# Three shared-expert products as seven products of halves, and routed sums moved ahead of a conditional block

## The chip, the cores and the metric

The kernel runs on one core of a Trainium2 chip. The metric is the device time of one execution in microseconds (us). The times of the kernel before are three runs: 1027.62, 1027.80 and 1028.35 us, median 1027.8 us. Times in tables of the trace are microseconds from the start of the profiled span.

TensorE (PE) multiplies matrices, VectorE (DVE), ScalarE (ACT) and GpSimd (POOL) do elementwise work, SyncE (SP) issues most of the DMAs, POOL issues the indirect ones (gathers). Each engine works through its own instructions in the order in which the program gives them; an instruction that waits holds up everything behind it on its engine.

## The reference, cut to what matters

Input is x of shape (4, 512, 512) in float32. A modulated layer norm leads to a block with a time mix and a channel mix, and then to a mixture of experts. Only this last part matters here:

```python
sh_mid = gelu(einsum('th,ehd->ted', xt, Wsh_up))          # 2 shared experts, 512 -> 256
shared_out = einsum('ted,edh->th', sh_mid, Wsh_down)      # 256 -> 512, summed over both
probs = softmax(xt @ W_router)
top_v, top_i = top_k(probs, 2)                            # of 16 routed experts
rt_mid = gelu(einsum('th,ehd->ted', xt, Wrt_up))
routed_out = einsum('ted,edh->th', rt_mid * gate[:, :, None], Wrt_down)
...
x = x + gb * (shared_out + routed_out)
```

## The kernel before, in words

A batch is 512 tokens, four row tiles of 128 (`NT = 4`), with `H = 512` features, `T = 512` tokens, half size `HT = 256`. The program runs: the time mix of the four batches, the channel mix of the four batches (its large products are already done as seven products of halves), and the experts. Nothing reorders the work: the order of every engine's instructions is the order of the Python code.

**Shared experts.** `shared_up(b)` computes, for the four 128-row pieces of the two experts' middle layer, four matmuls each with a 128x512 result, 16 in all, and a Gelu into a `mid` tile. `shared_down(b)` computes, for four row tiles, four matmuls with a 128x512 result, again 16 in all; `scaled_onto` (L1177, L1178) multiplies by the batch's gate row and adds onto x. Both are generators: each `yield` gives back control, so that their steps can be put between other work. Of the eight shared products, `shared_up(0)`, `shared_up(1)` and `shared_down(0)` are woven into the last channel mix. The other five belong to the part looked at here.

**Routed experts.** Tokens are sorted into slots of 128 rows, each with one expert's weights. 41 slots always run (`N_FIRST`), six more only if the device's count says so (the `tc.If` at L1426; it was not taken in this execution). A slot passes through five steps: `turn` (gathered rows are transposed, L1222, copied by DVE, L1224), `up` (8 records of 256-wide matmuls, Gelu), `turn_mid` (L1238, L1240), `down` (4 records of 512-wide matmuls, ACT copy), `keep` (a DMA stores the rows to `y_d`). Each step of slot s stands beside the previous step of slot s+1. Weights and rows are fetched three slots ahead.

**Fillers.** Every second pass of the slot loop from s = 22 on also runs one step of `groups`, which chains `shared_down(1)` and `shared_up(2)`, four steps each. In the passes s = 41 to 44, which drain the slots, it runs one step of `last_ups`, which is `shared_up(3)`. `gather(b, t)` fetches each token's two routed rows from `y_d` with two indirect DMAs; `routed(b, t)` combines them (ACT scales one, L1292; DVE L1293, then `scaled_onto`). For batches 0 and 1 this is done between the slots; `gather(2, ...)` is issued in the passes s = 43 and 44.

**The end.** After `last_ups` comes the conditional block, then `gather(3, ...)` (eight indirect DMAs on POOL), then the shared down products of batches 2 and 3. There `routed_and` (L1300, L1301) adds the two gathered rows straight to the product in PSUM, then `scaled_onto`, then a store. The very last row tile (b = 3, t = 3) has its routed part added earlier by `routed`, and its product is made in two halves of 256 columns in one PSUM bank (L1444), with a DVE multiply and add for each half (L1452, L1453) and a store of each half.

PSUM has eight banks, four with the tag "ps" and four with the tag "acc".

**The conditional block in the built program.** Every engine passes the `If`. On the path that is not taken, an engine waits until its own instructions so far are done, and then raises its count by what the block would have raised it by. The first matmul behind the block waits for DVE's count as it stands after this, that is, for a DVE that has itself finished everything ahead of the block and has passed it. This holds in the program before (where DVE's last instruction ahead of the block is the copy L1240 of slot 40) and in the changed one.

**The front.** In the time mix of batch 1, `weave` runs steps of `time_front(2)` between the steps of the main work; a plan says how many per main step. The step `n(3)` there makes the last normalized tile `xn_ln` (L219 on ACT) which PE then transposes (L226).

Of the kernel before, what the change touches and what calls it, by code (L numbers as in the profile page):

```python
# [10 lines left out]
AF = mybir.ActivationFunctionType  # L11
# [3 lines left out]
P = 128  # L15
# [29 lines left out]
def adaln_block(  # L45
# [1100 lines left out]
    def shared_up(b, halves=False):  # L1146
        mids[b] = []
        for wu, _ in shared:
            for m in range(ND):
                ps = bank(f"ps_up_sh_{b}_{len(mids[b])}")  # L1150
                for k in range(NK):
                    nc.tensor.matmul(  # L1152
                        ps, wu[:, k, m * P : (m + 1) * P], h3s[b][k], start=(k == 0), stop=(k == NK - 1)
                    )
                    if halves and k % 2:
                        yield
                act = row_tile(f"mid_{b}_{len(mids[b])}", (P, T))
                nc.scalar.activation(act, ps, AF.Gelu)
                mids[b].append(act)
                if not halves:  # L1160
                    yield
        h3s[b] = None

    def down_products(b, t, ps, js):
        for j in js:
            nc.tensor.matmul(  # L1166
                ps,
                mids[b][j][:, t * P : (t + 1) * P],
                shared[j // ND][1][:, j % ND, :],
                start=(j == 0),  # L1170
                stop=(j == len(mids[b]) - 1),
            )
# [115 lines left out]
    def routed(b, t):  # L1288

        g0, g1 = gates_of(b, t)  # L1290
        y0, y1 = got.pop((b, t))
        nc.scalar.activation(y1, y1, AF.Copy, scale=g1)  # L1292
        nc.vector.scalar_tensor_tensor(y0, y0, g0, y1, ALU.mult, ALU.add)  # L1293
        scaled_onto(b, t, y0)

    def routed_and(b, t, ps):

        g0, g1 = gates_of(b, t)
        y0, y1 = got.pop((b, t))
        nc.vector.scalar_tensor_tensor(y0, y0, g0, ps, ALU.mult, ALU.add)  # L1300
        nc.vector.scalar_tensor_tensor(y0, y1, g1, y0, ALU.mult, ALU.add)  # L1301
        scaled_onto(b, t, y0)
# [65 lines left out]
    for b in range(1, B):  # L1368
        if b + 1 < B:
            back = chained(lambda: time_front(b + 1))  # L1370
        else:
            wcr = load_w(wcr_t, "wcr")
            loaded[0] = load_keys(0, 0)
            back = front_and_sums()
            gas[0] = spread(GA, 0)
        weave(time_mix(b), back, (2, 1, 2, 1, 2) if b == 1 else ())
        drain(back)
# [27 lines left out]
    groups = chained(lambda: shared_down(1), lambda: shared_up(2))  # L1405
    last_ups = shared_up(B - 1)
    at = [slots_by(b) + 5 for b in range(B - 1)]
    for s in slots(0, N_FIRST, ready):
        if s >= slots_by(0) - 1 and (s - slots_by(0)) % 2:
            next(groups, None)  # L1410
# [13 lines left out]
    drain(last_ups)  # L1424
    n_used = nc.values_load(used[0:1, 0:1], min_val=0, max_val=N_SLOT)
# [4 lines left out]
    for b in (B - 2, B - 1):  # L1430
        for t in range(NT):
            ps = down_bank(b, t)
            if b == B - 1 and t == NT - 1:
                break
            down_products(b, t, ps, range(4))
            if b == B - 1 and t == NT - 2:
                routed(b, NT - 1)
            routed_and(b, t, ps)
            store_out(b, t)

    last = x1s[B - 1][NT - 1]
    for at in (slice(0, HT), slice(HT, H)):
        for j in range(4):
            nc.tensor.matmul(  # L1444
                ps[:, at],
                mids[B - 1][j][:, (NT - 1) * P :],
# [4 lines left out]
        add = row_tile(f"add_last_{at.start}")  # L1451
        nc.vector.tensor_mul(add[:, at], ps[:, at], gbs[B - 1][:, at])  # L1452
        nc.vector.tensor_add(last[:, at], last[:, at], add[:, at])  # L1453
# [45 lines left out]
```

## Time and profile before

| | |
|---|---|
| median of the runs | 1027.8 us (1027.62 to 1028.35, 3 runs) |
| the profiled execution | 1028.34 us, of it a span of 1026.5 us; 1.84 us lie around the span |
| busy in the span | PE 98%, DVE 60%, ACT 31%, POOL 33% |
| PE waiting, the two largest sums | L226 for ACT's `xn_ln` 6.5 us (5 times), L1444 for DVE's `add_last` 3.3 us (once) |
| granted TensorE clock | 0.997 over the span |
| DMA | 178 GB/s over the span; 382 GB/s and PE busy throughout at 800 to 825 us, 268 to 326 GB/s at 875 to 950 us |

The trace can be read line by line: a line of the timeline gives the start, the duration, the engine, the source line, the operation with output and inputs, the shape, and how many instructions of the kind followed each other; in brackets stands how long the engine had been idle, and what ended that. A float32 matmul leaves two records. The durations of single matmuls overlap, so the pace of PE is read from starts, not from durations.

### The profile page before, as it was taken

The numbers are of one execution on the slowest core, as the hardware profiler recorded it, in microseconds if no ns is written. First come the engines' busy times: TensorE is split into PE (matmuls) and PEld (weight loads), VectorE is DVE, ScalarE is ACT, GpSimd is POOL, SyncE is SP. The second block draws the span as 40 slices with busy tenths as digits, with TensorE's granted clock in tenths as the row PEclk, the third lists the DMA queues.
The fourth block names the chain that finished last, engine by engine and source line by source line (L and its number), as shares of the span: only waits on it lengthen the run. The fifth ranks groups of instructions, "written<-read, shape, count | busy, mean of one in ns | idle before, by whom it ended". The sixth has DMA issues, their size and how long they took to land. (4 is left out here: it accounts for less than half of the span.)

```text
span 1026.5 us, 11651 instructions
## 1 busy us (share of the span) xinstructions
PE 1003.0 (98%) x3930; PEld 685.8 (67%) x3930; DVE 616.8 (60%) x1181; ACT 319.8 (31%) x530; POOL 342.3 (33%) x324
## 2 busy tenths in 40 slices
PE   7999999999999999999999999999998999999997
PEld 2444444444688888888888888888646676666643
DVE  5787887797665736848757587428654222233426
ACT  1765645653222305320262203220021222122310
POOL 2463563514354105620266006520104221232160
PEclk9999999999999999999999999999999999999999
DMA  9600401352069562365226534650536999899762
GB/s 328 247 0 2 125 19 42 103 192 86 1 225 349 178 233 83 121 232 178 88 76 215 195 133 175 240 180 1 185 123 187 365 382 383 270 321 316 266 194 83
DMA packets 96765, 182.83 MB, mean 178 GB/s; under 512 B 7528, under 2 KB 50280, under 8 KB 92608
## 3 DMA queue, kind: packets, MB, share of 16 engines
q1 hardware_dynamic: 90864, 162.92, 45.6%
q0 software_dynamic: 5840, 19.14, 5.8%
q8 instruction: 32, 0.52, 0.2%
q14 instruction: 29, 0.24, 0.1%
HBM read 149.75 MB, written 32.29 MB: 177 GB/s over the span
## 5 line engine op out<-in xcount | busy, mean ns | idle before, releaser
L199 POOL TENSOR_TENSOR rstd_ln<-rstd_ln,minus_half 128x1 f32<-128x1 f32 x64 | 42.9, 672 | 199.5 <-DVE rstd_ln L198 182.5
L782 PE MATMUL ps_y<-wval,a 128*128 128x256 f32 x384 | 86.0, 380 | 0.0
L1207 POOL DMA_INDIRECT xg<-h_d,token x41 | 39.5, 963 | 127.9 <-PE ps_xt L1222 44.8
L782 PEld LDWEIGHTS ps_y<-wval,a 128*128 128x128 f32 x384 | 72.3, 190 | 12.0 <-issue 2.5
L1230 PE MATMUL ps_up<-wrt,xt 128*128 128x256 f32 x328 | 78.0, 381 | 0.3 <-ACT act L1232 0.2
L1246 PE MATMUL ps_down<-wrt,at 128*128 128x512 f32 x164 | 77.2, 593 | 0.0
L1230 PEld LDWEIGHTS ps_up<-wrt,xt 128*128 128x128 f32 x328 | 59.1, 190 | 8.0 <-DVE xt L1224 1.0
L1224 DVE COPY xt<-ps_xt 128x512 f32<-128x512 f32 x41 | 28.2, 689 | 56.2 <-PE ps_xt L1222 42.1
L711 PE MATMUL ps_ky<-T,keys_hi 128*128 128x256 f32 x256 | 60.6, 380 | 0.0
L711 PE MATMUL ps_kx<-mix_ln,keys_lo 128*128 128x256 f32 x256 | 60.5, 379 | 0.0
L357 PE MATMUL ps_o<-wo,av 128*128 128x512 f32 x128 | 57.4, 597 | 2.4 <-DVE x L427 1.2
L352 PE MATMUL ps_r<-mix_ln,wr 128*128 128x512 f32 x128 | 57.6, 593 | 0.8 <-issue 0.8
L782 PE MATMUL ps_z<-wval,a 128*128 128x256 f32 x256 | 57.9, 380 | 0.0
L352 PE MATMUL ps_v<-mix_ln,wv 128*128 128x512 f32 x128 | 57.5, 592 | 0.0
L782 PE MATMUL ps_x<-wval,a 128*128 128x256 f32 x256 | 57.2, 379 | 0.0
L1152 PE MATMUL ps_up_sh<-h,wsh 128*128 128x512 f32 x128 | 57.2, 593 | 0.0
L394 DVE RECIPROCAL p<-p 128x512 f32<-128x512 f32 x16 | 53.6, 3353 | 0.6
L1166 PE MATMUL ps_down_sh<-wsh,mid 128*128 128x512 f32 x120 | 53.1, 595 | 0.3 <-PEq L1426 0.3
L711 PEld LDWEIGHTS ps_kx<-mix_ln,keys_lo 128*128 128x128 f32 x256 | 48.5, 190 | 6.9 <-issue 0.5
L711 PEld LDWEIGHTS ps_ky<-T,keys_hi 128*128 128x128 f32 x256 | 48.3, 190 | 6.8 <-DVE ku L749 0.4
L782 PEld LDWEIGHTS ps_z<-wval,a 128*128 128x128 f32 x256 | 48.1, 190 | 6.8 <-issue 0.6
L782 PEld LDWEIGHTS ps_x<-wval,a 128*128 128x128 f32 x256 | 48.2, 190 | 6.3
(260 smaller groups left out, 1845.3 us busy)
## 6 DMA issues: line engine op xcount, KB each, us to landing
wrt<-in_rt_up_dram SPq DMA_DIRECT2D x41, 512.0 KB
wrt<-in_rt_down_dram SPq DMA_DIRECT2D x41, 512.0 KB
wval<-sums_d SPq DMA_DIRECT2D x16, 1024.0 KB
wval<-in_wval_t_dram SPq DMA_DIRECT2D x12, 1024.0 KB
keys_lo<-keys_d SPq DMA_DIRECT2D x12, 1024.0 KB
y_d<-y SPq DMA_DIRECT2D x41, 256.0 KB
keys_hi<-keys_d SPq DMA_DIRECT2D x12, 768.0 KB
mod<-mod_d SPq DMA_DIRECT2D x22, 256.0 KB
```

The lines of the kernel that those rows point to most:

```text
L199: nc.gpsimd.tensor_tensor(rstd, rstd, minus_half, ALU.pow)
L352: nc.tensor.matmul(ps, w[:, k, m * P : (m + 1) * P], acts[k], start=(k == 0), stop=(k == NK - 1))
L357: nc.tensor.matmul(ps, acts[k][:, t * P : (t + 1) * P], w[:, k, :], start=(k == 0), stop=(k == NK - 1))
L394: nc.vector.reciprocal(p, p)
L711: nc.tensor.matmul(ps[:, c * HT : (c + 1) * HT], w[:, k, c * P : (c + 1) * P], acts[k], start=(fresh and c == 0 and k == 0), stop=(c == 1 ...
L782: nc.tensor.matmul(ps[:, j * HT : (j + 1) * HT], acts[p][:, c, j * P : (j + 1) * P], w[:, i, :], start=(fresh and i == 0 and j == 0), stop ...
L1152: nc.tensor.matmul(ps, wu[:, k, m * P : (m + 1) * P], h3s[b][k], start=(k == 0), stop=(k == NK - 1))
L1166: nc.tensor.matmul(ps, mids[b][j][:, t * P : (t + 1) * P], shared[j // ND][1][:, j % ND, :], start=(j == 0), stop=(j == len(mids[b]) - 1),)
L1207: nc.gpsimd.indirect_dma_start(out=xg, out_offset=None, in_=h3_d, in_offset=bass.IndirectOffsetOnAxis(ap=token[:, s : s + 1], axis=0),)
L1224: nc.vector.tensor_copy(xt.rearrange("p k t -> p (k t)"), ps)
L1230: nc.tensor.matmul(ps[:, :D], xt[:, k, :], wu[:, k, :], start=(k == 0), stop=(k == NK - 1))
L1246: nc.tensor.matmul(ps, at[:, j, :], wd[:, j, :], start=(j == 0), stop=(j == ND - 1))
```

## The change

1. `shared_down(1)`, `shared_up(2)` and `shared_up(3)` become `shared_down_seven` and `shared_up_seven`: each is cut into 2 x 2 halves and computed with seven products of halves (four 256-wide matmuls each, 28 in all) in place of eight (16 matmuls of width 512), with DVE additions of the partial results.
2. The sums of halves that this needs are made ahead: `shared_sums()`, eight DVE additions of 128x512, in the pass s = 3 of the slot loop; `shared_down_terms(1)` (four of 128x512) at s = 19, `shared_up_terms(2)` (eight of 128x256) at s = 27, `shared_up_terms(3)` (eight of 128x256) at s = 37.
3. In `shared_down_seven`, DVE multiplies by the gate row, and POOL adds the halves of 128x256 onto x.
4. The middle tiles of batches 0 and 1 are written per half of the tokens: two Gelus of 256 columns instead of one of 512.
5. The plan of the weave in the time mix of batch 1 becomes (2, 2, 1, 2).
6. `routed(2, t)` for all four t, with DVE also doing the scaling (`tensor_scalar`), moves ahead of the conditional block. `routed_and` goes: behind the block, each product gets a `scaled_onto` alone, and `routed(3, t)` (scaling on ACT) follows the store of each tile of batch 2.
7. The two halves of the last row tile get a PSUM bank each.

```diff
     def shared_up(b, halves=False):
-        mids[b] = []
+        mids[b] = [[row_tile(f"mid_{b}_{t}_{f}", (P, ND, HT)) for f in range(E_SH)] for t in range(2)]
...
-                act = row_tile(f"mid_{b}_{len(mids[b])}", (P, T))
-                nc.scalar.activation(act, ps, AF.Gelu)
+                for t in range(2):
+                    nc.scalar.activation(mids[b][t][f][:, m, :], ps[:, t * HT : (t + 1) * HT], AF.Gelu)
...
+    def shared_sums():
...
+        add(ups, "S1", "A21", "A22", ALU.add)
+        add(ups, "S2", "S1", "A11", ALU.subtract)
+        add(ups, "S3", "A11", "A21", ALU.subtract)
+        add(ups, "S4", "A12", "S2", ALU.subtract)
+        add(downs, "T1", "B12", "B11", ALU.subtract)
+        add(downs, "T3", "B22", "B12", ALU.subtract)
+        add(downs, "T2", "B22", "T1", ALU.subtract)
+        add(downs, "T4", "B21", "T2", ALU.subtract)
...
+    def seven(name, product, A, Bs, use):
+        X = bank(f"{name}_x")
+        product(X, A["A11"], Bs["B11"], True)
+        c1 = copied(f"{name}_c1", X)
+        Y = bank(f"{name}_y", "acc")
+        product(Y, A["S2"], Bs["T2"], True)
+        u = row_tile(f"{name}_u")
+        nc.vector.tensor_add(u, c1, Y)
+        yield
+        Z = bank(f"{name}_z", "acc")
+        product(Z, A["S1"], Bs["T1"], True)
+        c5 = copied(f"{name}_c5", Z)
+        nc.vector.tensor_add(c5, c5, c1)
+        product(X, A["A12"], Bs["B21"], False)
+        use(0, 0, X)
+        yield
+        product(Y, A["S3"], Bs["T3"], False)
+        nc.vector.tensor_add(c5, c5, Y)
+        use(1, 1, c5)
+        product(Z, A["S4"], Bs["B22"], False)
+        nc.vector.tensor_add(u, u, Z)
+        use(0, 1, u)
+        yield
+        product(Y, A["A22"], Bs["T4"], False)
+        nc.vector.tensor_add(c1, c1, Y)
+        use(1, 0, c1)
+        yield
...
+    def shared_up_seven(b):
...
+        def use(f, t, v):
+            act = row_tile(f"mid_{b}_{t}_{f}")
+            nc.scalar.activation(act, v, AF.Gelu)
...
+    def shared_down_seven(b):
...
+        def use(i, j, v):
+            at = slice(j * HT, (j + 1) * HT)
+            add = row_tile(f"add_sh_{b}_{i}_{j}", (P, 2, HT))
+            row = gbs[b][:, None, at].broadcast_to([P, 2, HT])
+            nc.vector.tensor_tensor(add, v.rearrange("p (t o) -> p t o", t=2), row, ALU.mult)
+            for t in range(2):
+                xt = x1s[b][2 * i + t][:, at]
+                nc.gpsimd.tensor_add(xt, xt, add[:, t, :])
...
-    def routed(b, t):
+    def routed(b, t, engine=None):
         g0, g1 = gates_of(b, t)
         y0, y1 = got.pop((b, t))
-        nc.scalar.activation(y1, y1, AF.Copy, scale=g1)
+        if engine is nc.vector:
+            nc.vector.tensor_scalar(y1, y1, g1, None, ALU.mult)
+        else:
+            nc.scalar.activation(y1, y1, AF.Copy, scale=g1)
         nc.vector.scalar_tensor_tensor(y0, y0, g0, y1, ALU.mult, ALU.add)
         scaled_onto(b, t, y0)
...
-        weave(time_mix(b), back, (2, 1, 2, 1, 2) if b == 1 else ())
+        weave(time_mix(b), back, (2, 2, 1, 2) if b == 1 else ())
...
-    groups = chained(lambda: shared_down(1), lambda: shared_up(2))
-    last_ups = shared_up(B - 1)
+    groups = chained(lambda: shared_down_seven(1), lambda: shared_up_seven(2))
+    last_ups = shared_up_seven(B - 1)
...
     for s in slots(0, N_FIRST, ready):
+        if s == AHEAD:
+            shared_sums()
+        for when, terms, n in (
+            (slots_by(0) - 4, shared_down_terms, 1),
+            (slots_by(0) + 4, shared_up_terms, 2),
+            (N_FIRST - 4, shared_up_terms, 3),
+        ):
+            if s == when:
+                terms(n)
...
     drain(last_ups)
+    for t in range(NT):
+        routed(B - 2, t, nc.vector)
     n_used = nc.values_load(used[0:1, 0:1], min_val=0, max_val=N_SLOT)
     with tc.If(n_used > N_FIRST):
         drain(slots(N_FIRST, N_SLOT))
     for t in range(NT):
         gather(B - 1, t)
     for b in (B - 2, B - 1):
-        for t in range(NT):
+        for t in range(NT if b < B - 1 else NT - 1):
             ps = down_bank(b, t)
-            if b == B - 1 and t == NT - 1:
-                break
             down_products(b, t, ps, range(4))
-            if b == B - 1 and t == NT - 2:
-                routed(b, NT - 1)
-            routed_and(b, t, ps)
+            scaled_onto(b, t, ps)
             store_out(b, t)
+            if b < B - 1:
+                routed(B - 1, t)

     last = x1s[B - 1][NT - 1]
     for at in (slice(0, HT), slice(HT, H)):
+        ps = bank(f"ps_last_{at.start}", "acc")
```

## The prediction

> **What bounds the kernel now.** I read the busy shares, then PE's timeline among the slots and at the end, then DVE's beside it. The page's shares and two groups (count | busy us, mean ns | idle before):
>
> ```profile
> PE 1003.0 (98%) x3930; PEld 685.8 (67%) x3930; DVE 616.8 (60%) x1181; ACT 319.8 (31%) x530; POOL 342.3 (33%) x324
> L1230 PE MATMUL ps_up<-wrt,xt 128*128 128x256 f32 x328 | 78.0, 381 | 0.3 <-ACT act L1232 0.2
> L1152 PE MATMUL ps_up_sh<-h,wsh 128*128 128x512 f32 x128 | 57.2, 593 | 0.0
> ```
>
> PE is busy 1003.0 of 1026.5 us: time falls only where PE has less to do or waits less. The mean ns are latencies that overlap; the pace stands in PE's timeline (start, duration):
>
> ```profile
> 947.86 3.60 PE L1152 MATMUL ps_up_sh<-h,wsh 128*128 128x512 f32 x8
> 951.29 0.60 PE L1222 MATMUL ps_xt<-ident,xg 128*128 128x128 f32 x4
> 951.73 1.89 PE L1230 MATMUL ps_up<-wrt,xt 128*128 128x256 f32 x8
> 953.46 0.38 PE L1238 MATMUL ps_at<-ident,act 128*128 128x128 f32 x2
> ```
>
> Start to start, eight 512-wide records take 951.29 − 947.86 = 3.43 us (0.429 each), eight 256-wide ones 953.46 − 951.73 = 1.73 us (0.215 each): half the width is half the time. PE's timeline at the start, in the front and at the end:
>
> ```profile
> 1.94 7.36 PE L136 MATMUL ps_warm<-ones,ident 128*128 128x512 f32 x12 [1.94 <-POOL ones L123]
> ...
> 116.77 0.33 PE L226 MATMUL ps_t_ln<-ident,xn_ln 128*128 128x128 f32 x1 [1.81 <-ACT xn_ln L219]
> ...
> 982.65 7.03 PE L1152 MATMUL ps_up_sh<-h,wsh 128*128 128x512 f32 x16
> 989.98 24.27 PE L1166 MATMUL ps_down_sh<-wsh,mid 128*128 128x512 f32 x56 [0.30 <-PEq L1426]
> 1014.09 1.89 PE L1444 MATMUL ps_down_sh<-wsh,mid 128*128 128x256 f32 x8
> 1019.25 3.43 PE L1444 MATMUL ps_down_sh<-wsh,mid 128*128 128x256 f32 x8 [3.27 <-DVE add_last L1452]
> ```
>
> PE crosses the conditional block in 0.30 us, and near the end loses 3.27 us to DVE; the eight records after that wait take 3.43 us, twice their pace. DVE's timeline:
>
> ```profile
> 788.61 0.41 DVE L1240 COPY at<-ps_at 128x256 f32<-128x256 f32 x1
> 788.94 0.68 DVE L1224 COPY xt<-ps_xt 128x512 f32<-128x512 f32 x1
> ...
> 973.62 0.75 DVE L1293 SCALAR_TENSOR_TENSOR y<-y,gates,y 128x512 f32<-128x512 f32 x1 [1.47 <-ACT y L1292]
> 974.40 0.69 DVE L1177 TENSOR_TENSOR add<-y,mod 128x512 f32<-128x512 f32 x1
> 975.13 0.69 DVE L1178 TENSOR_TENSOR x<-x,add 128x512 f32<-128x512 f32 x1
> 975.98 0.42 DVE L1240 COPY at<-ps_at 128x256 f32<-128x256 f32 x1 [0.16 <-PE ps_at L1238]
> 993.69 0.75 DVE L1300 SCALAR_TENSOR_TENSOR y<-y,gates,ps_down_sh 128x512 f32<-128x512 f32 x1 [17.28 <-PE ps_down_sh L1166]
> ...
> 1023.18 0.42 DVE L1453 TENSOR_TENSOR x<-x,add_last 128x256 f32<-128x256 f32 x1
> ```
>
> DVE has nothing from 976.40 to 993.69, so the first matmul behind the block, which waits for a DVE that has passed it, found it done long before.
>
> **The change part by part.** E is the moment when PE ends its last matmul ahead of the block (before: 989.68).
>
> *Seven products.* Before, a product is 16 matmuls, 32 records of 0.429 = 13.73 us; after, 28 matmuls of 256, 56 records × 0.2145 = 12.01. Three times 1.72: **−5.16 us**. Their DVE, ACT and POOL work lies under PE: in the slots at 797 us an `xt` copy ends 3.2 us before PE needs it, and the largest step adds four DVE operations of 0.69 = 2.8 us within a slot of 7.5. The terms at s = 19 (4 × 0.69 = 2.8) and s = 27 and 37 (8 × 0.42 = 3.4) start behind an `at` copy, with some 3 us to the next transposes and 3.2 more behind them; without this cover they would cost 2.8, 3.4 and 3.4. The split Gelus (0.60 for 512 columns) sit on an ACT that is 31% busy. Weights arrive at 383 GB/s from 825 to 850 us, the filler slots need 268 to 326, so shorter fillers meet no transfer. POOL's adds (128x512 takes 1.3 to 1.45, so some 0.7 each for half, eight) delay row fetches that run three slots ahead. Nothing for these.
>
> *`shared_sums`.* Eight DVE additions stand behind the copy that ends at 789.03 and ahead of the `xt` copy that ran at 788.94. Pitches: 0.73 where one needs the one before (974.40 to 975.13), 0.61 otherwise; 2 × 0.73 + 5 × 0.61 + 0.69 = 5.2, so the copy ends at about 794.3 + 0.69 + 0.1 = 795.1, while PE started `up(4)` at 792.96. Behind it only `at(2)` is queued, which is in time. **+2.2 us** (0 if DVE comes earlier here, 2.7 at 0.73 throughout).
>
> *The weave.* `n(3)` comes a step earlier, ahead of a reciprocal (L394, 3.35 us) and of exponents that held it up. The wait at 116.77 can fall from 1.81 to 0; the moved exponents may give one ACT operation (0.7) back. **−1.2 us** (−1.8 to +0.7).
>
> *Routed sums ahead of the block.* DVE's last addition of `shared_up(3)` ends at E + 0.75; then come four times `tensor_scalar`, `scalar_tensor_tensor`, mul, add. The last three take 0.78 + 0.73 + 0.61 = 2.12. The trace has no wide `tensor_scalar`: bounds are 0.35 (L1053, 128x128) and 0.78 (L1293's pitch, one more tensor read); it shares its kind with the one and its width with the other, so 0.57. 4 × 2.69 = 10.8. The gathered rows are there: eight gathers start at 975.96 with a pitch of 1.25 us and land some 3.6 us after their start, the last near 988.3, before E. DVE ends at E + 11.55 and crosses the block in 0.30 to 0.6; PE, which before resumed at E + 0.30, resumes at E + 12.0. **+11.7 us** (10.6 to 12.9). Queued behind that matmul is everything left on PE. POOL's last gathers ahead of tile 3 wait for early operations of these sums only, and land before they are needed.
>
> *PE restarts cold.* The wait of 3.27 us was followed by 3.43 us for what takes 1.72; the twelve first matmuls of the run took 7.36 us for 12 × 0.429 = 5.15, a loss of 2.2. After 12 us of idle I take **+1.9** (0 to 2.2).
> In the trace the granted clock of 1019 to 1023 us is 0.58. The Trainium skill, TensorE: Matmul & The Clock Gate, "The HAM clock gate", says that an idle window of about 3.4 us halves PE's clock and that about 3.4 us of sustained work bring it back; it advises against such gaps, and so against this one. By its figures this term would be an estimated 1.7, and the sum 0.2 lower. The same skill, VectorE: DVE Perf Modes, "The perf-mode tier table", lets a float32 `tensor_scalar` run at twice the rate of `tensor_tensor`; that would be an estimated 0.42 here, 0.6 less over four; no row shows it.
>
> *The end.* Seven 512-wide products and two halves follow on PE (7 × 3.43 + 2 × 1.72 = 27.45). Per tile of batch 2 DVE has mul, add, STT, mul, add, 0.73 + 0.61 + 0.78 + 0.73 + 0.61 = 3.46, as long as PE's 3.43; tiles of batch 3 need 1.34, so DVE catches up, and with a bank for each half the wait of 3.27 and the slow half (3.43 − 1.72) go: **−4.98**. Last additions and store stay (1022.68 to 1026.5).
>
> Sum: 1026.5 − 5.16 + 2.2 − 1.2 + 11.7 + 1.9 − 4.98 = 1030.96 for the span, with 1.84 around it 1032.8, against 1028.34 for the profiled execution: +4.5. That execution is 0.54 above the median 1027.8, so **1032.2 us**. All low ends give −5.16 + 0 − 1.8 + 10.6 + 0 − 4.98 = −1.3, or 1026.5; all high ends −5.16 + 2.7 + 0.7 + 12.9 + 2.2 − 4.98 = +8.4, or 1036.2.
>
> **The rivals.**
> A. PE crosses the block without DVE, and the routed sums fill DVE's idle 17.28 us for nothing on PE. For it: that hole. Against: the count that the first matmul waits for. DVE then becomes the end's bound: from E + 0.75, 10.8 + 4 × 3.46 + 3 × 1.34 + 2 × 0.87 = 30.4, and 2.9 for the store: E + 34.1, where before the end was at 1026.5 − 989.68 = E + 36.8. Then −5.16 + 2.2 − 1.2 − 2.7 = −6.9: 1020.9. Faster.
> B. The stall is there, but what lies around it comes out at the low ends (copy in time, no cold restart, cheap sums): 1026.5 to 1029.5, no change or nearly.
> C. 256-wide records cost their 0.38 us: 3 × (56 × 0.380 − 32 × 0.593) = +6.9 in place of −5.16, 1044. Against it: the starts above.
> D. The filler steps' DVE work does hold `xt` copies: 2.8 + 3.4 + 3.4 on top, up to 1041. Against it: PE waits nowhere at 875 to 950 us, with DVE busy 7 to 10 of every 25 us.
>
> **How the numbers follow.** A measurement of this kernel tells 0.2%, 2.1 us, from no change. My forecast, slower by more than that, has 0.64; A 0.19; B 0.13 (0.10 within 0.2%, 0.03 faster); C 0.01; D 0.03. So faster 0.22, same 0.10, slower 0.68. The forecast's own range is 1029.9 to 1036.2. To leave out no more than 2 in 10 the range reaches down through B into the upper part of A: 1022.0 to 1036.5.
>
> **What would show it.** Right: an idle of some 12 us on PE ahead of the first L1166-like matmul behind the block, ended by DVE; DVE busy without a gap through it; records at twice their pace for about 3.5 us after it; 12.0 us of PE for each of the three products; a wait of about 2 us near 793; no wait at the last half. Wrong: if PE resumes within 1 us of its last matmul (A), if PE waits among the filler slots (D), or if seven products take longer than 13.7 us (C).

## The result, and the profile after

The changed kernel took 1043.98 us (median of 5 runs, 1040.24 to 1047.84), the kernel before 1027.8 us on the same chip (5 runs, 1027.49 to 1029.79): a ratio of 1.0148, 95% interval 1.0127 to 1.0170. It is slower by 16 us, and above the range that was forecast. The profiled execution took 1043.98 us, of it a span of 1042.3 us, with a mean granted clock of 0.985.

The page's shares of the changed kernel, and PE's waits in it (waiting operation, what it waited for: us in total, times, longest):

```profile
PE 1005.1 (96%) x4002; PEld 702.8 (67%) x4002; DVE 645.3 (62%) x1231; ACT 325.9 (31%) x547; POOL 348.0 (33%) x332
```

```profile
PE ps_down_sh L1297 <- ACT y L1426: 12.0, 1, 12.0
PE ps_up L1361 <- ACT act L1363: 4.8, 1, 4.8
PE ps_t_ln L226 <- ACT xn_ln L219: 4.8, 5, 1.5
PE ps_up L1361 <- DVE xt L1355: 2.5, 1, 2.5
```

PE has fewer columns to multiply and is still busy for as long as before (1005.1 against 1003.0), so some of its work ran at a lower clock; and there are two waits among the slots, L1361 for the Gelu of a routed slot (L1363) and for the `xt` copy of a slot (L1355), of which the kernel before had the first for 0.2 us and the second not at all. To see where the time went I cut the span at three points of PE's timeline: the first transposes of the slots, E (the end of the last matmul ahead of the conditional block), and the first matmul behind the block.

| us | to the first slot | slots, to E | idle at the block | from there to the end | span |
|---|---|---|---|---|---|
| before | 776.1 | 213.6 | 0.3 | 36.5 | 1026.5 |
| forecast | 774.9 | 210.6 | 12.0 | 33.4 | 1031.0 |
| changed | 776.5 | 219.2 | 12.0 | 34.6 | 1042.3 |

The idle at the block is as forecast; the slots are 8.6 us longer than forecast, and the other two columns together 2.8. PE's timeline at the end of the changed kernel (start, duration, and in brackets the idle before):

```profile
993.79 1.89 PE L1231 MATMUL up_sh_y<-h_T,wsh 128*128 128x256 f32 x8
...
1007.69 27.28 PE L1297 MATMUL ps_down_sh<-wsh,mid 128*128 128x512 f32 x56 [12.01 <-ACT y L1426]
1034.81 3.62 PE L1580 MATMUL ps_last<-wsh,mid 128*128 128x256 f32 x16
```

The 56 records behind the block take 1034.81 − 1007.69 = 27.1 us; before, 1014.09 − 989.98 = 24.1. The releaser named in brackets, an ACT operation, is only the last that ended; DVE's timeline shows who holds the block:

```profile
995.72 0.69 DVE L1221 TENSOR_TENSOR up_sh_c<-up_sh_c,up_sh_y 128x512 f32<-128x512 f32 x1
996.32 0.55 DVE L1424 TENSOR_SCALAR y<-y,gates 128x512 f32<-128x512 f32 x1
996.90 0.75 DVE L1427 SCALAR_TENSOR_TENSOR y<-y,gates,y 128x512 f32<-128x512 f32 x1
...
1006.32 0.69 DVE L1309 TENSOR_TENSOR x<-x,add 128x512 f32<-128x512 f32 x1
1014.41 0.69 DVE L1308 TENSOR_TENSOR add<-ps_down_sh,mod 128x512 f32<-128x512 f32 x1 [7.40 <-PE ps_down_sh L1297]
```

L1221 is the last addition of `shared_up(3)`, which waits for the product that PE ended at E. The four routed sums run from 996.32 to 1007.01, without a gap, and 0.68 us after the last of them PE goes on. Then DVE has nothing to do for 7.40 us.

The rest is among the slots. From one stretch of the changed kernel's timelines (POOL, PE, DVE, ACT; the last two lines are from a second stretch):

```profile
904.64 1.41 POOL L1290 TENSOR_TENSOR x<-x,add_sh 128x256 f32<-128x256 f32 x2 [5.83 <-DVE add_sh L1287]
912.82 1.89 PE L1231 MATMUL up_sh_y<-h_T,sh_S 128*128 128x256 f32 x8
920.47 0.69 DVE L1204 TENSOR_TENSOR up_sh_u<-up_sh_c,up_sh_y 128x512 f32<-128x512 f32 x1 [10.47 <-PE ps_xt L1353]
923.35 0.38 ACT L1363 ACTIVATE act<-ps_up 128x256 f32<-128x256 f32 x1 [8.08 <-remote]
924.06 2.47 PE L1361 MATMUL ps_up<-wrt,xt 128*128 128x256 f32 x5 [4.81 <-ACT act L1363]
...
960.81 0.69 DVE L1221 TENSOR_TENSOR up_sh_c<-up_sh_c,up_sh_y 128x512 f32<-128x512 f32 x1 [8.63 <-PE ps_xt L1353]
962.15 3.42 PE L1361 MATMUL ps_up<-wrt,xt 128*128 128x256 f32 x8 [2.46 <-DVE xt L1355]
```

The addition L1204 needs the product that PE ended at about 914.55 and a copy that ACT ended at 914.0, and yet it starts at 920.47, after 10.47 us of idle DVE; ACT is idle for 8.08 us in the same stretch. PE works through what it has, and then waits 4.81 us. I call such a stretch a hold. The bracket at L1204 names PE: a signal of PE ended the wait. The trace's record of these signals shows how late they are. PE's timeline ends seven groups of matmuls between 912.98 and 919.25, and goes on to the next at its usual pace; the first is signalled at 913.32, the second, the product that L1204 needs, only at 920.37, and the other five within 923.24 to 923.49. So DVE and ACT are not slow at their own work: they are told late that PE has gone on. During all of this POOL issues twelve gathers in a row, from 906.20 to 920.92, one every 1.25 us: they had piled up behind the half additions L1290, for which POOL had waited 5.83 us. The same happens again beside nine gathers, with DVE idle for 8.63 us and a wait of 2.46 us on PE. What these waits cost beyond themselves is seen in the stretches behind them (window, its length; busy time and count of PE, PEld, DVE, ACT, POOL; granted clock, DMA share, GB/s):

```profile
922.06:924.06 2.00, 0.00 (x1) 0.04 (x1) 1.97 (x4) 0.71 (x2) 0.00 (x0) 0.50 0.99 389
926.06:928.06 2.00, 2.00 (x8) 1.53 (x7) 1.58 (x3) 0.15 (x1) 0.00 (x0) 0.50 1.02 220
962.15:964.15 2.00, 2.00 (x6) 1.62 (x7) 2.00 (x7) 0.77 (x3) 0.00 (x0) 0.60 1.03 385
1009.69:1011.69 2.00, 2.00 (x4) 0.85 (x3) 0.00 (x0) 0.29 (x1) 0.00 (x0) 0.50 0.00 0
1013.69:1015.69 2.00, 2.00 (x6) 0.95 (x5) 1.24 (x2) 0.00 (x0) 0.00 (x0) 0.98 0.00 0
```

The granted clock is 0.50 to 0.60 for some 4 us behind each of the two waits, and 0.50 for 6 us behind the block. At half the clock 4 us lose some 2, an estimate; with the two waits, 7.3 us, that makes some 11 us. The slots are 8.6 us longer than forecast, and the forecast held 2.2 us for `shared_sums` that did not come (below).

### The profile page after: what moved, and what is told of

It reads as the page before. It is cut to its first block, busy times and chain, and to the rows that moved or that the text cites. A ratio compares the mean times of both kernels' runs of the same rounds, so it can differ in the third digit from the quotient of the medians.

```text
span 1042.3 us, 11868 instructions
## 1 busy us (share of the span) xinstructions
PE 1005.1 (96%) x4002; PEld 702.8 (67%) x4002; DVE 645.3 (62%) x1231; ACT 325.9 (31%) x547; POOL 348.0 (33%) x332
## 5 line engine op out<-in xcount | busy, mean ns | idle before, releaser
L1361 PE MATMUL ps_up<-wrt,xt 128*128 128x256 f32 x328 | 81.3, 392 | 7.4 <-ACT act L1363 4.8
L1361 PEld LDWEIGHTS ps_up<-wrt,xt 128*128 128x128 f32 x328 | 61.0, 196 | 16.1 <-ACT act L1363 5.0
L1297 PE MATMUL ps_down_sh<-wsh,mid 128*128 128x512 f32 x88 | 41.7, 633 | 12.0 <-ACT y L1426 12.0
L1355 DVE COPY xt<-ps_xt 128x512 f32<-128x512 f32 x41 | 28.2, 687 | 36.5 <-PE ps_xt L1353 34.7
L219 ACT ACTIVATE xn_ln<-x,nm_ln,rstd_ln 128x512 f32<-128x512 f32 x32 | 25.3, 810 | 78.5 <-DVE nm_ln L212 78.5
```

The costliest lines, as they stand in the source:

```text
L219: nc.scalar.activation(n, src, AF.Identity, scale=rstd, bias=nm)
L1297: nc.tensor.matmul(ps, mid_of(b, j, t), shared[j // ND][1][:, j % ND, :], start=(j == 0), stop=(j == E_SH * ND - 1),)
L1355: nc.vector.tensor_copy(xt.rearrange("p k t -> p (k t)"), ps)
L1361: nc.tensor.matmul(ps[:, :D], xt[:, k, :], wu[:, k, :], start=(k == 0), stop=(k == NK - 1))
```

## The experiments

The runs were made on four chips, in five groups (on which chip the first measurement was made is not on record); each ratio is against runs of the kernel before on the same chip in the same group. "Waits among the slots" are PE's waits between its first slot and E.

### The two large parts alone (second chip)

**tail_only**: the kernel before with parts 6 and 7 of the change, the shared products left as they were.

```diff
     drain(last_ups)
+    for t in range(NT):
+        routed(B - 2, t, nc.vector)
     n_used = nc.values_load(used[0:1, 0:1], min_val=0, max_val=N_SLOT)
...
-            routed_and(b, t, ps)
+            scaled_onto(b, t, ps)
             store_out(b, t)
+            if b < B - 1:
+                routed(B - 1, t)
```

> The kernel before with parts 6 and 7 alone (routed sums of batch 2 ahead of the conditional block, a bank for each last half). Theory, the wait at the block: in the changed kernel the stretch from PE's last matmul ahead of the block (995.51) to the end (1042.3) is 46.8 us, before it is 1026.5 - 989.68 = 36.8; so +10.0, 1037.8 us, with an idle of 11 to 12 us on PE ended by DVE. Rival, the idle comes from the late gathers or from the seven products: then no idle above 1 us, and the end is 2 to 5 us shorter, about 1023 to 1026 us.

Measured: 1025.86 us (10 runs) against 1026.32, ratio 0.9996 (0.9986 to 1.0007). The expectation missed. DVE's timeline in this kernel, and PE's:

```profile
980.41 0.59 DVE L1293 TENSOR_SCALAR y<-y,gates 128x512 f32<-128x512 f32 x1 [5.15 <-DMA y<-y_d,pos_i]
...
991.07 0.69 DVE L1178 TENSOR_TENSOR x<-x,add 128x512 f32<-128x512 f32 x1
```

```profile
981.50 7.03 PE L1152 MATMUL ps_up_sh<-h,wsh 128*128 128x512 f32 x16
992.10 24.27 PE L1166 MATMUL ps_down_sh<-wsh,mid 128*128 128x512 f32 x56 [3.57 <-DVEq L1423]
```

Without the seven products nothing that waits for PE stands ahead of the sums on DVE. They begin when the gathered rows have landed, at 980.41, eight microseconds ahead of E, and only 3.57 us of them stick out behind E. So the idle of 12 us belongs to neither part alone: part 6 puts four sums ahead of the point for which PE waits at the block, and part 1 puts an addition that waits for E ahead of the sums.

**seven_only**: the kernel before with parts 1 to 4 of the change (the diff of those parts), and its own end.

> The kernel before with parts 1 to 4 alone (the three seven-product steps, their sums, the halved Gelus). Theory, the new steps leave PE without cover while DVE and ACT are held during the bursts of gathers: 5.2 us of matmuls saved, some 11 lost to two waits among the slots and the slow clock behind them, +5 to +6, 1033 us. Rival, the waits of the changed kernel among the slots were an accident of that execution or came from the other parts: -5.2, about 1022.6 us.

Measured: 1022.9 us (6 runs), ratio 0.9963 (0.9950 to 0.9975). My theory, that the slots' waits come with the seven products wherever they run, missed; the rival had the time. But no run on this chip has a hold, so this one does not tell what the products cost where there are holds. There is no new wait among the slots here; the block costs 1.07 us, for the last addition. The slots, to E, take 206.45 us, against 211.2 in **tail_only**: 4.75 us less, of the 5.16 forecast for the matmuls, so that some 0.4 is left for `shared_sums`, by one execution of each.

**block_free**: the changed kernel, with the routed sums directly behind the block.

```diff
-    for t in range(NT):
-        routed(B - 2, t, nc.vector)
     n_used = nc.values_load(used[0:1, 0:1], min_val=0, max_val=N_SLOT)
...
         gather(B - 1, t)
+    for t in range(NT):
+        routed(B - 2, t, nc.vector)
```

> The changed kernel with the four routed sums of batch 2 put directly behind the conditional block. Theory, PE waits at the block for DVE: PE now resumes within 1.5 us; DVE becomes the bound of the end: 10.7 for the four sums, 4 x 3.45, 3 x 1.34, 2 x 0.87 and 2.9 for the store give 34.5 us from PE's last matmul ahead of the block, where the changed kernel takes 46.8; so 12.3 us less than the changed kernel, about 1031 to 1032 us. Rival, the sums cost the same wherever they stand because the end is bound by DVE: 1040 us or more.

Measured: 1018.01 us, ratio 0.9913 (0.9897 to 0.9930). PE's timeline:

```profile
982.96 24.27 PE L1297 MATMUL ps_down_sh<-wsh,mid 128*128 128x512 f32 x56 [1.07 <-DVEq L1561]
1007.07 3.62 PE L1580 MATMUL ps_last<-wsh,mid 128*128 128x256 f32 x16
```

The idle fell from 12.0 to 1.07 us and the 56 records take 24.1 us again: no slow clock behind the block. With two lines moved past the block the changed kernel is, on this chip, faster than the one before.

**own_banks**: the kernel before with part 7 alone.

```diff
     for at in (slice(0, HT), slice(HT, H)):
+        ps = bank(f"ps_last_{at.start}", "acc")
         for j in range(4):
```

> The kernel before with a PSUM bank for each half of the last row tile, nothing else. Theory: the wait of 3.27 us and the slow half behind it go; the second half ends near 1017.5, DVE's last two operations follow its backlog and end near 1020.5, and with 2.9 for the store the span is 1023.4, so -3.1, 1024.7 us. Rival, PE stays behind DVE's backlog anyway: within 1 us of before.

Measured: 1023.33 us, ratio 0.9961 (0.9947 to 0.9975), 3.0 us less than before, as expected.

### The changed kernel once more, and smaller parts (third chip)

**after_again**: the changed kernel, unedited.

> The changed kernel once more, nothing edited, beside the others on one chip. Theory, the two waits among the slots (11 us with the slow clock behind them) belong to the state of DMA traffic and semaphores in that measurement, as seven_only and block_free hold the same steps without them: they are gone, the wait of 12 us at the block stays, 1018.0 + 12.3 = about 1030 us. Rival, they belong to this program: 1040 us or more, with waits of 2 to 5 us on PE at 915 to 965.

Measured: 1030.59 us (4 runs, 1029.68 to 1032.28), ratio 1.0047 (1.0028 to 1.0065), with a span of 1028.7. On this chip the same program is 13 us faster than in the first measurement. PE's waits, the largest, and the timelines of PE, DVE and ACT at the place of the first measurement's first hold:

```profile
PE ps_down_sh L1297 <- DVEq L1563: 12.0, 1, 12.0
```

```profile
911.41 1.89 PE L1231 MATMUL up_sh_y<-h_T,sh_S 128*128 128x256 f32 x8
913.40 0.69 DVE L1204 TENSOR_TENSOR up_sh_u<-up_sh_c,up_sh_y 128x512 f32<-128x512 f32 x1 [4.82 <-ACT y L1426]
915.50 0.38 ACT L1363 ACTIVATE act<-ps_up 128x256 f32<-128x256 f32 x1 [2.15 <-PE ps_up L1361]
```

Here L1204 starts 0.3 us after its product, and no wait among the slots is above 0.8 us. POOL has its pile of gathers here too, 14 between 904.79 and 922.22: the pile alone does not make a hold. The block is as before, 11.95 us.

**weave_only**: the kernel before with part 5 alone.

```diff
-        weave(time_mix(b), back, (2, 1, 2, 1, 2) if b == 1 else ())
+        weave(time_mix(b), back, (2, 2, 1, 2) if b == 1 else ())
```

> The kernel before with the plan of the weave (2, 2, 1, 2) alone. By the prediction -1.2 us (-1.8 to +0.7). In the changed kernel's trace the first wait for the last normalized tile is gone but PE began the first slot at 776.49 against 776.09 before, which speaks for nothing gained: rival, -0.3 to +0.7.

Measured: 1026.39 us (11 runs) against 1026.14, ratio 1.0004 (0.9995 to 1.0013): no gain. The wait of 1.81 us is gone, and PE's timeline has these instead:

```profile
209.11 0.33 PE L226 MATMUL ps_t_ln<-ident,xn_ln 128*128 128x128 f32 x1 [0.38 <-ACT xn_ln L219]
...
214.32 3.70 PE L357 MATMUL ps_o<-wo,av 128*128 128x512 f32 x8 [1.01 <-DVE x L427]
```

The second was 0.50 before. At these two places PE lost again what it had gained: the stall did not go, it moved some 95 us down the line.

**sums_first** and **split_sums**: the changed kernel with all four, or two, of the routed sums ahead of DVE's last addition of `shared_up(3)` (in **split_sums** the other two go behind the block).

```diff
         if s >= N_FIRST:
+            if s == N_FIRST + 3:
+                for t in range(NT):
+                    routed(B - 2, t, nc.vector)
             next(last_ups)
...
-    for t in range(NT):
-        routed(B - 2, t, nc.vector)
```

> The changed kernel with the four routed sums of batch 2 still ahead of the block, but ahead of DVE's last addition of shared_up(3) too. Theory, the 12 us at the block are DVE's sums started only after PE's last matmul, since the last addition stands ahead of them on DVE: now they follow the gathers, the last of which lands 0.4 us after PE's last matmul, so DVE is through 3.9 us after it and PE waits some 4 us instead of 12: about 7.8 us less than the changed kernel on the same chip. Rival, the wait is set by the block itself and not by the order ahead of it: the same as the changed kernel.

> block_free with the first two of the four routed sums put ahead of DVE's last addition of shared_up(3), where DVE is idle, the other two behind the block. Theory, DVE's backlog decides the end of block_free by 1.6 us (PE done at 1010.5, DVE at 1013.1 where 0.9 behind PE would do): PE resumes as early as there and DVE has 5.3 us less to do behind the block, so 1.6 us less than block_free, 1016.4 us. Rival, the sums ahead of the block hold PE up again: 1018 us or more.

Measured: 1028.87 us, ratio 1.0024 (1.0015 to 1.0034), and 1023.78 us, ratio 0.9971 (0.9960 to 0.9983). **sums_first** gained less than expected, and **split_sums** took 7.4 us more than expected. DVE's timeline in **sums_first**, and PE's:

```profile
981.74 0.69 DVE L1217 TENSOR_TENSOR up_sh_u<-up_sh_u,up_sh_z 128x512 f32<-128x512 f32 x1 [1.04 <-PE up_sh_z L1231]
982.35 0.48 DVE L1424 TENSOR_SCALAR y<-y,gates 128x512 f32<-128x512 f32 x1
```

```profile
993.81 26.01 PE L1297 MATMUL ps_down_sh<-wsh,mid 128*128 128x512 f32 x56 [10.38 <-DVEq L1564]
```

The sums stood ahead of the last addition but behind those of the third step, which wait for PE as well; they began at 982.35, and 10.38 us of the idle stayed (5.11 in **split_sums**). DVE has to be given the sums at a place where it waits for the gathered rows, not for PE.

### How to keep the gain, and the pile of gathers (second chip again)

**after_third** and **block_free2** are the changed kernel and **block_free** unedited. **spread** is the changed kernel with the gathers of batches 0 and 1 issued in every second pass:

```diff
-            if 0 <= s - at[b] < NT:
-                gather(b, s - at[b])
-            if 0 <= s - at[b] - 2 < NT:
-                routed(b, s - at[b] - 2)
-            if 0 <= s - at[b] - 3 < NT:
-                store_out(b, s - at[b] - 3)
+            for since, step in ((0, gather), (2, routed), (3, store_out)):
+                d = s - at[b] - since
+                if 0 <= d < 2 * NT and d % 2 == 0:
+                    step(b, d // 2)
```

**early_two** has two sums ahead of the third step of `shared_up(3)`, and two behind the block:

```diff
         if s >= N_FIRST:
+            if s == N_FIRST + 2:
+                for t in range(2):
+                    routed(B - 2, t, nc.vector)
             next(last_ups)
```

> The changed kernel a third time, unedited, to see which of its two measurements so far (1044.0 with two waits among the slots, 1030.6 without) this chip repeats. Theory, the waits come with the chip: 1030 us without them, or 1040 and more with DVE or ACT idle for 8 to 10 us during a burst of gathers; the time and the idle stretches go together. Rival, time and idle stretches don't go together.

> The changed kernel with the gathers of batches 0 and 1 in every second pass of the slot loop in place of every pass. Theory, where DVE and ACT are held during long bursts of gathers on POOL: the burst of 12 to 14 becomes several of at most 4 to 6, and if this chip shows the waits in the changed kernel, they are gone or shorter here (some 11 us less); if it doesn't show them, the same time within 1 us. Rival, the bursts have nothing to do with it: the same waits in both.

> block_free with the first two of the four routed sums ahead of the third step of shared_up(3) on DVE, where DVE was idle for 3.8 us and more; in split_sums they stood behind the additions of that step, which wait for PE, and PE lost 5.1 us. Theory: the gathered rows of the first tile are there 6 to 7 us ahead of PE's last matmul, so both sums end before it, PE resumes within 1.5 us, and DVE's backlog behind the block shrinks by 5.3 us: 1.6 us less than block_free. Rival, the rows land too late or the later additions of shared_up(3) become late: PE waits 2 us or more at the block, not better than block_free.

> block_free once more, unedited, beside early_two on one chip: 1018 us. If this chip shows waits among the slots in the changed kernel, the same here, some 11 us more.

Measured, with a ratio each: **after_third** 1030.23 us, 1.0045 (1.0029 to 1.0061), again without the holds; **spread** 1035.08 us, 1.0088 (1.0067 to 1.0108); **early_two** 1019.64 us, 0.9931 (0.9915 to 0.9948); **block_free2** 1019.70 us, 0.9932 (0.9915 to 0.9948).

**spread** tells nothing of the holds, since the chip had none to take away; the first pile was still of twelve gathers. It took 4.9 us more than **after_third**. At the block the last gathers came later, the sum `routed(1, 3)` with them, at 986.03 on DVE, ahead of the last addition, and PE idled 14.05 us, 2.1 more; another 2.2 us lie ahead of the first slot, where nothing was changed, and 1.0 in the slots. **early_two** gained nothing over **block_free2**, against 1.6 us expected. Its timelines of DVE and PE say why:

```profile
983.41 0.68 DVE L1214 TENSOR_TENSOR up_sh_c<-up_sh_c,up_sh_y 128x512 f32<-128x512 f32 x1
984.14 1.99 PE L1231 MATMUL up_sh_y<-h_T,wsh 128*128 128x256 f32 x8 [1.61 <-DVE up_sh_c L1214]
```

The end did shorten, from 33.0 to 31.6 us after the first matmul behind the block; but L1214, now behind two sums, reads the bank that PE's next product overwrites, and PE waits for it.

### How much a hold costs each kernel (fourth chip)

**after_fourth** is the changed kernel unedited. **early_one** is **early_two** with one sum ahead of the third step and three behind the block. **hold_before** and **hold_block_free** are the kernel before and **block_free** with DVE work whose results nothing uses, at one pass of the slots:

```diff
     for s in slots(0, N_FIRST, ready):
+        if s == 36:
+            held = row_tile("held")
+            for _ in range(3):
+                nc.vector.reciprocal(held, gbs[0])
```

> The changed kernel, unedited, once more: 1030 us as in after_again and after_third, or 1040 and more as in the first measurement. Theory: where it is 1040 and more, DVE and ACT show idle stretches of 8 to 10 us near 910 to 923 and 952 to 961 that end with PE's late signal, and PE waits 2 to 5 us after each; where it is 1030, none.

> block_free with the first one of the four routed sums ahead of the third step of shared_up(3). Two sums there made DVE's addition of that step 1.4 us late, and the next matmul, which overwrites what it reads, waited 1.6 us (early_two); one sum ends near 980.5, before PE ends that step's first product, so no wait. Theory: PE resumes behind the block as in block_free, DVE's backlog of 4.6 us there is made up by the three tiles of batch 3 (3 x 2.1), and the end is PE's: 31.4 us from the resumption in place of 33.0, 1.6 us less than block_free, 1016.4 to 1018 us. Rival, DVE's backlog still decides: less than 0.5 us gained.

> The kernel before with three extra DVE reciprocals (10.05 us, result unused) in pass 36 of the slot loop, ahead of the last step of shared_up(2): a hold of DVE like the one seen in the first measurement. Theory, cover: PE has some 1.4 us of the running product, 3.43 of the filler and 4.5 of two slots' other steps, 9.4 in all, before it needs a copy from DVE, which comes some 10.7 after: +1 to +1.5 us. Rival, any hold of this length costs its whole length or most of it: +5 us or more.

> block_free with the same hold at the same pass. Theory, cover: the filler there is the fourth step of the seven products, 1.72 us in place of 3.43, and DVE has an addition of 0.69 ahead of the copy: the cover is 7.7 and the copy comes 11.4 after, so +3.7 us, some 2.4 more than the same hold costs the kernel before; with the slow clock behind a wait of that length up to +5.5. Rival, the seven products don't make the slots more fragile: the same cost in both within 1 us.

**after_fourth**: 1041.05 us against 1027.63, ratio 1.0128 (1.0103 to 1.0154). The holds are back. Its timelines of DVE, ACT and PE:

```profile
917.73 0.69 DVE L1204 TENSOR_TENSOR up_sh_u<-up_sh_c,up_sh_y 128x512 f32<-128x512 f32 x1 [8.35 <-PE ps_at L1369]
922.69 0.38 ACT L1363 ACTIVATE act<-ps_up 128x256 f32<-128x256 f32 x1 [8.19 <-remote]
923.13 3.78 PE L1361 MATMUL ps_up<-wrt,xt 128*128 128x256 f32 x8 [4.49 <-ACT act L1363]
```

The same instructions are held as in the first measurement, and the same matmul waits. **early_one**: 1027.29 us, ratio 0.9995 (0.9985 to 1.0006); at the block it idles 1.07 us, but it has waits of 4.45 and 1.68 us among the slots, and on this chip its gain is gone.

The kernel before has such holds too, in its first profile already. Its timelines of ACT, DVE and PE there:

```profile
954.67 0.60 ACT L1158 ACTIVATE mid<-ps_up_sh 128x512 f32<-128x512 f32 x1 [6.01 <-PE ps_at L1238]
955.43 0.69 DVE L1224 COPY xt<-ps_xt 128x512 f32<-128x512 f32 x1 [8.67 <-remote]
956.22 1.97 PE L1230 MATMUL ps_up<-wrt,xt 128*128 128x256 f32 x8 [0.23 <-ACT act L1232]
```

DVE stands for 8.67 us and ACT for 6.01, while POOL issues gathers from 942.55 to 953.5; PE loses 0.23 us. In the changed kernel the hold at the same stage, with the same nine gathers beside it and 8.63 us long on DVE, cost PE 2.46. So a hold of that size was nearly free before and cost 2 to 5 us after. **hold_before** and **hold_block_free** measure this with a hold of known length, three reciprocals, 10.05 us. **hold_before**: 1030.20 us, ratio 1.0022 (1.0012 to 1.0031). **hold_block_free**: 1034.45 us, ratio 1.0068 (1.0048 to 1.0089). The wait behind the hold, in PE's timeline of the one and of the other:

```profile
956.37 1.97 PE L1230 MATMUL ps_up<-wrt,xt 128*128 128x256 f32 x8 [1.45 <-issue]
```

```profile
962.42 3.78 PE L1361 MATMUL ps_up<-wrt,xt 128*128 128x256 f32 x8 [3.71 <-DVE xt L1355]
```

As expected, the same hold costs PE 1.45 us in the one and 3.71 in the other, and the eight records behind the longer wait take 3.78 us in place of 1.97. The seven products leave PE less to do between a slot's transposes and its first matmuls (1.72 us of products in the last step, 3.43 before), and so less cover, and DVE has an addition ahead of the copy, 0.5 us. The totals fit less neatly, since **hold_block_free** also has this chip's own wait of 4.73 us, and **block_free** was not run here; only the two lines are compared. That the late signals of PE cost more for the same reason is inferred from this pair.

### One early sum, and a smaller pile of gathers (fifth chip)

**early_one2** is **early_one** unedited. **dve_adds** is **early_one** with the half additions of `shared_down(1)` on DVE, so that POOL's gathers do not pile up behind them:

```diff
                 xt = x1s[b][2 * i + t][:, at]
-                nc.gpsimd.tensor_add(xt, xt, add[:, t, :])
+                nc.vector.tensor_add(xt, xt, add[:, t, :])
```

> early_one with the eight half additions of shared_down(1) onto x on DVE in place of POOL. Theory, pile-up: on POOL the last of them waits for DVE (5.8 us idle in the changed kernel) and the gathers behind them come out in one burst of 12 to 14; without them POOL is free of DVE, the burst starts earlier and is split, and where the chip shows the wait for ACT of some 4.5 us near 919 to 923 it is shorter or gone, 4 to 6 us less than early_one2 on the same chip; where the chip shows no such wait, the same as early_one2 within 0.5 us, since DVE has slack in the slots. Rival, the burst isn't what holds DVE and ACT: the same waits in both.

> early_one once more. Theory: on a chip without the waits among the slots 1016.4 to 1018 us, 1.6 less than block_free (1018.0 and 1019.7 there); on a chip with them 1027 us as measured.

Measured: **dve_adds** 1016.80 us (4 runs), ratio 0.9906 (0.9889 to 0.9922); **early_one2** 1017.03 us, ratio 0.9913 (0.9896 to 0.9930). The pile of 14 gathers became one of six, with a pause of 0.72 us in it, and one of five; a later one of nine stayed. On this chip nothing is held, so the two are equal; what **dve_adds** does on a chip with holds was not tried. PE's timeline of **early_one2**:

```profile
983.75 24.27 PE L1297 MATMUL ps_down_sh<-wsh,mid 128*128 128x512 f32 x56 [1.07 <-DVEq L1563]
```

From there to the end it takes 31.55 us, 1.5 less than **block_free**, where one sum more stands on DVE behind the block. In the whole time this gain does not show: the ratio of **block_free** on the second chip was 0.9913 and 0.9932.

## Why the prediction was right in direction and wrong in size

The stages of the unedited changed kernel in its four measurements, cut as above:

| us | to the first slot | slots, to E | idle at the block | to the end | span |
|---|---|---|---|---|---|
| forecast | 774.9 | 210.6 | 12.0 | 33.4 | 1031.0 |
| first measurement | 776.5 | 219.2 | 12.0 | 34.6 | 1042.3 |
| **after_fourth** | 776.3 | 215.8 | 12.0 | 34.5 | 1038.5 |
| **after_again** | 776.2 | 206.5 | 12.0 | 34.1 | 1028.7 |
| **after_third** | 776.1 | 206.4 | 11.9 | 34.0 | 1028.5 |

- **The step that failed** is "Nothing for these", the cover of the filler slots. The prediction set the work that the change itself adds to DVE (2.8 to 3.4 us) against some 3 us to the next transposes and 3.2 behind them, which is enough, and **after_again** and **after_third** show it: no such wait there. It did not set the cover against the holds that DVE and ACT have in this stretch anyway, in some measurements. The trace of before had one of 8.67 us, at a cost of 0.23 us to PE, and "PE waits nowhere at 875 to 950 us", the argument against rival D, took a wait that was absent for a wait that could not come. The seven products took away the cover (1.45 us against 3.71 for one and the same hold put in), and where the term was nothing, the slots became 9.3 and 12.7 us longer in the two measurements that have holds than in **after_again** (215.8 and 219.2 against 206.5). The slots of the kernel before were some 2.4 us longer with holds than those of **tail_only**, the same slots, without (213.6 against 211.2). The prediction had POOL's additions only "delay row fetches"; they also piled up twelve gathers, but that this has a part in the holds is not shown.
- **What makes a hold is open.** The profiled executions are of two kinds. In six (the kernel before, the first measurement, the four on the fourth chip) the next signal of PE on record comes more than 1 us after the timeline's end of a group among the slots 19 to 25 times; in the other fourteen it is never later than 0.02 us. The holds fall within piles of gathers on POOL, while weights stream; but **after_again** has a pile of 14 without one, so the pile is not enough. That POOL's additions cause it was only argued: **dve_adds**, which makes the pile smaller, ran on a chip without holds. Nor is it settled whether the recording of the trace has a part: the six also lack some of PE's signals (650 in the first measurement, 660 in **after_again**), and every run on record was traced (each has a span and a granted clock).
- **Routed sums ahead of the block**: right, 12.0 us of idle in each of the four profiles; four sums took 1007.01 − 996.32 = 10.7 us (forecast 10.8). A single `tensor_scalar` takes 0.48 to 0.55 us, within its bounds, and starts 0.52 us ahead of its successor in a run of them: below the 0.57 taken. The Trainium skill, VectorE: DVE Perf Modes, "The perf-mode tier table", was the source of the estimated 0.42; the measurement lies between the two and decides. What the forecast did not say is that the 12 us need part 1 as well (**tail_only**: 3.57).
- **Seven products**: right; **seven_only** is 3.4 us faster than before with 1.07 us of idle at the block in it. So C fell.
- **`shared_sums`**: mis-sized, +2.2 for some 0.4. In the trace of before DVE was late at this place and PE lost 1.6 us there; in **after_again** the additions start 3.6 us earlier than worked out, and PE does not wait.
- **The weave**: mis-sized, −1.2 for nothing (**weave_only**, 1.0004). The step looked at the wait that goes and not at the next one down the line.
- **PE restarts cold**: the sign right, the size 1.9 for 3.0 (and 2.5 in **after_again**, 26.6 us for 24.1). The clock stayed at 0.50 for 6 us, where 3.5 were forecast. The Trainium skill, TensorE: Matmul & The Clock Gate, "The HAM clock gate", has the clock halved by an idle window of some 3.4 us and brought back by some 3.4 us of work; here the way back took 6 us (5 in **after_again**), and a wait of 2.46 us was enough to bring the clock down to 0.60, while behind the 1.68 us of **early_one** it stayed at 1.00.
- **The end**: right. The wait at the last half is gone, and **own_banks** alone gains 3.0 us.
- **The rivals**: A fell, since PE does not cross the block without DVE. B fell; in the measurements without holds the slots come out near their low end, but not the restart. That those, at 1030.2 and 1030.6 us, lie within the forecast's own range is in part luck: in **after_again** the slots are 4.1 us shorter than forecast, and 1.3 us more ahead of them and 0.7 more at the end make up for half of it. That C named 1044, the time of the first measurement, is chance: in **after_again** eight records of 256 columns still take 1.73 us (909.68 to 911.41), 0.216 each and not 0.38. D was right in what waits (L1361 for `xt`, and for `act`), and wrong in why: not the filler steps' own work, but holds that they no longer cover.

## What to carry to other kernels

A late engine that costs nothing in a profile may only just be covered: when a change shortens work on the engine that sets the pace, look for the long idle stretches of the other engines that this work covered, and charge what the new cover leaves bare. Work that is moved ahead of a point where all engines meet is paid in full if something ahead of it in its queue waits for the engine that sets the pace; place it behind what arrives early. Before a loss is put down to a change, run the same program on a second chip.

## What the runs showed that I had not expected

- The same program took 1030.2 and 1030.6 us on two chips, 1041.1 on a third and 1044.0 in the first measurement, while the kernel before moved by 1.7 us (1026.1 to 1027.8).
- DVE and ACT stood for 5 to 10 us at a time, both together, because signals of PE reached them some 5 to 8 us after PE's timeline ends the work.
- The granted clock fell to 0.60 behind a wait of 2.46 us, and took 6 us of work at 0.50 to come back after 12 us of idle.
